# Eleven groups of a graph attention take their keys and values from node rows gathered early instead of from the table

## The chip, the cores and the metric

The kernel runs on one core of a Trainium2 chip. The metric is the device time in microseconds from the start of the program to its end. The engines are TensorE (PE, with its weight loads shown as PEld), VectorE (DVE), ScalarE (ACT), GpSimd (POOL) and SyncE (SP). Each works through its own queue in order, and they meet at semaphores.

## The reference

A graph of 3125 nodes (128 features, 8 heads of 16) has 100,000 edges, sorted by their destination, each of one of 5 relations. For every relation the edges attend within their destination node:

```python
for r in range(R):
    mask = edge_types == r
    q = jnp.einsum('eh,khd->ekd', x_dst, W_Q[r])
    k = jnp.einsum('eh,khd->ekd', x_src, W_K[r])
    v = jnp.einsum('eh,khd->ekd', x_src, W_V[r])
    logits = (q * k).sum(-1) / scale + attn_bias[r][None, :]
    masked_logits = jnp.where(mask[:, None], logits, NEG)
    max_v = jax.ops.segment_max(masked_logits, dst, num_segments=n)
    max_v = jnp.maximum(max_v, NEG)
    exp_l = jnp.where(mask[:, None], jnp.exp(masked_logits - max_v[dst]), 0.0)
    sum_exp = jax.ops.segment_sum(exp_l, dst, num_segments=n)
    attn = exp_l / (sum_exp[dst] + 1e-12)
    out = out + jax.ops.segment_sum(attn[:, :, None] * v, dst, num_segments=n)
out = out.reshape(n, HIDDEN)
out = out @ out_proj_w.T + out_proj_b
h = out + node_embeddings
mu = h.mean(-1, keepdims=True)
var = ((h - mu) ** 2).mean(-1, keepdims=True)
return (h - mu) / jnp.sqrt(var + LN_EPS) * ln_gamma + ln_beta
```

The caller adds the node features to this and normalizes once more. All is in 32-bit floats.

## The kernel before

The edges are cut into 196 groups of 512 (four tiles of 128 edges), the nodes into 25 blocks of 128. One block covers about 8 groups.

**First stage.** A loop over the 25 blocks makes a table `kv_d` in DRAM with the keys and values of every node under every relation. `turn` transposes a block of node rows, `table` multiplies it with the weights `wkv` in three f32 products (L312), ACT and DVE copy the results to SBUF (L316, L318) and SP stores them. Between the blocks stand pieces of bookkeeping, placed by the dictionary `side`: `begins` spreads the first destination of every group, `rows_of` finds for every node the row of sorted destinations in which it begins by comparing it with the first element of all 200 rows of 500, `in_row` gathers these rows (L341), and `count` counts on ACT how far into its row the node begins (L349). `keys_a` to `keys_c` and `along` make the indices `idx` and the keys of the edges.

**Second stage.** A loop over steps `k`. In step `k` one group `g` gets its logits, and one earlier group `v` gets its weights and sums. For a group:

- `gather` (POOL) fetches the 512 rows of `kv_d` with four indirect DMAs, three steps ahead (`AHEAD`), into one of `KVB` = 24 buffers.
- `fetch` (SP) loads the keys and a window of query rows; `spot` (DVE) makes a one-hot matrix of them; `spread_q` (PE, L603) multiplies the two, which gives each edge the query of its destination.
- `logits` (DVE, L616 and L617) multiplies keys and queries and reduces over each head; `store_logits` (SP) writes the result to `lg_d`.
- Later, for `v`: `spread_m` (PE) gives each edge its maximum, `less_max` (DVE) subtracts it, `exps` (ACT) exponentiates, `weigh` (DVE, L710) multiplies the values, `places` (ACT, L728 and L731) makes the one-hot matrix by destination, `sums` (PE, L744 to L754) adds up by destination, with the part that `carry` (ACT) took over from the group before, and `norm` (DVE) and `by_node` (ACT) divide and store.

For a block of nodes, once all of its groups have logits (step `full_step[b]`), `maxima_load` (POOL, L629) gathers the logits `ell` of each node from `lg_d` one step later. In the steps `ready[b]` - 5 and - 4, where `ready[b]` is `full_step[b]` plus `LAG` = 8 (6 for the last three blocks), `maxima` reduces them: ACT copies them by head into the PSUM tile `by_head` (L641), DVE forms `mine` (L643), `wl` (L656) and the maxima `mx` (L662). `store_m`, `fetch_m` then take the maxima to the groups, whose sums begin in step `ready[b]`. Sums run one group per step; `CATCH_UP` names five late groups that take two steps each, so that sums gain on the logits. `project`, `residual`, `roots` and `norms` finish a block, `queries` makes the query rows of a coming one.

The order on each engine is that of the program: in each step first the SP loads and stores, then POOL's gathers and `maxima_load`, then `residual`, `by_node` and `carry`, `spread_m`, `sums`, `spread_q`, and then the vector work, with `maxima`, `project`, `roots`, `norms` and `queries` last.

Of the kernel before, what the change touches and what calls it, by code (L numbers as in the profile page):

```python
# [17 lines left out]
P = 128  # L18
# [29 lines left out]
CATCH_UP = (186, 188, 190, 192, 194)  # L48
# [6 lines left out]
LAG = 8  # L55
SR = 500
NSR = E // SR
KVB = 24
# [58 lines left out]
def windowed_path(  # L117
# [13 lines left out]
    key_d = dram.tile([NGR, GE], BF16, name="key_d")  # L131

# [17 lines left out]
    wq = keep("wq", [P, R, H])  # L150

# [15 lines left out]
    nc.vector.memset(xn[:, NT - 1, :], 0.0)  # L167
    fr = load.tile([1, NGR + NSR], I32, name="fr")
# [16 lines left out]
    nc.sync.dma_start(xn[:, :4, :], x[: 4 * P].rearrange("(i p) h -> p i h", p=P))  # L185
# [7 lines left out]
    def load_rows(name, a, pad):  # L193
        t = load.tile([HG, 2, GE], I32, name=name)
        nc.vector.memset(t[:, 1, :], pad)
        nc.scalar.dma_start(t[:, 0, :], a[: HG * GE].rearrange("(g i) -> g i", i=GE))
        nc.scalar.dma_start(
            t[: HR - 1, 1, :], a[HG * GE : (NGR - 1) * GE].rearrange("(g i) -> g i", i=GE)
        )
        rest = E - (NGR - 1) * GE  # L200
        nc.gpsimd.dma_start(
            t[HR - 1 : HR, 1, :rest], a[(NGR - 1) * GE :].rearrange("(g i) -> g i", g=1)
        )
        return t
# [30 lines left out]
    mid = iota("mid", [[P * E // N, NT]], NT)  # L235
    five = iota("five", [[R, WN]], WN, mult=-1)
# [21 lines left out]


    wkv = load.tile([P, R, 2, H], F32, name="wkv")  # L260
# [14 lines left out]
    firsts = load.tile([P, NGR + NSR], F32, name="firsts")  # L275
    frf = load.tile([1, NGR + NSR], F32, name="frf")

    def begins():
        nc.vector.tensor_copy(frf, fr)
        fp = pps.tile([P, NGR + NSR], F32, name="fp", tag="tr", bufs=2)  # L280
        nc.tensor.matmul(fp, ones[0:1, :], frf, start=True, stop=True)
        nc.vector.tensor_copy(firsts, fp)
        nc.vector.tensor_copy(first, frf[:, :NGR])
        nc.vector.tensor_scalar_mul(first5, frf[:, :NGR], float(R))
        nc.vector.tensor_tensor(
            nkey[:, T, 1:], firsts[:, 1:NGR], firsts[:, : NGR - 1], op=ALU.subtract
        )
        nc.vector.tensor_scalar(
            nkey[:, T, 1:], nkey[:, T, 1:], float(R), row_of, op0=ALU.mult, op1=ALU.subtract
        )  # L290
# [35 lines left out]
    def rows_of(c0, c1):  # L326
        less = work.tile([P, 5, NSR], BF16, name="less", bufs=1)
        nc.vector.tensor_tensor(
            less,
            firsts[:, None, NGR:].to_broadcast([P, 5, NSR]),  # L330
            node[:, c0:c1, None].to_broadcast([P, 5, NSR]),
            op=ALU.is_lt,
        )
        g = grp[:, c0:c1]
        nc.vector.tensor_reduce(g, less, AX.X, ALU.add)
        nc.vector.tensor_scalar(g, g, 1.0, 0.0, op0=ALU.subtract, op1=ALU.max)
        nc.vector.tensor_copy(grp_i[:, c0:c1], g)
# [97 lines left out]
    def checks():  # L435
# [19 lines left out]
        1: [lambda: rows_of(0, 5)],  # L455
        2: [lambda: rows_of(5, 10), lambda: rows_of(10, 15)],
        3: [lambda: rows_of(15, 20)],
        4: [lambda: rows_of(20, NT)],
        5: [keys_a],
        6: [keys_c],  # L460
        7: [lambda: along(kvrow, 0, put_idx)],
        8: [lambda: along(kvrow, 1, put_idx)],
        9: [keys_b],
        11: [lambda: along(keyr, 0, put_key)],
        12: [lambda: along(keyr, 1, put_key)],
        13: [lambda: along(typr, 0, put_typ)],
        14: [lambda: along(typr, 1, put_typ)],
        16: [sorted_rows],
        18: [sorted_ends],
        21: [starts],  # L470
        23: [checks],
    }
    rows, counted = {}, 0
    xT = {b: turn(b) for b in range(2)}
    for b in range(NT):
        if b + 2 < NT:
            xT[b + 2] = turn(b + 2)
        table(b, xT.pop(b))
        for f in side.get(b, ()):
            f()  # L480
        while len(rows) < min(NT, 5 * b) and len(rows) - counted < 8:
            rows[len(rows)] = in_row(len(rows))
        for n in range(2):
            if b >= 3 and counted < len(rows):
                count(counted, rows[counted])
                counted += 1

# [39 lines left out]
    def gather(g):  # L527
        kv = kvs_[g % KVB]
        for t in range(T):
            nc.gpsimd.indirect_dma_start(  # L530
                out=kv[:, t, :], out_offset=None, in_=kv_d[:, :],
                in_offset=bass.IndirectOffsetOnAxis(ap=idx[:, t, g : g + 1], axis=0),
            )
# [49 lines left out]

    def fetch(g):
# [28 lines left out]
    def logits(g):  # L613
        kv, lg = kvs_[g % KVB], live["lg", g]
        prod = flow.tile([P, T, H], F32, name="prod")
# [20 lines left out]
    def maxima(b, c0, c1):  # L636
# [17 lines left out]
        wl = late_flow.tile([P, RH, HEADS, D], F32, name="wl", bufs=1)  # L654
# [200 lines left out]
    def lag(b):  # L855

        return LAG if b < NT - 3 else LAG - 2

# [18 lines left out]
    root_at[NT] = root_at[NT - 1] + 2  # L877

# [32 lines left out]
    for k in range(root_at[NT] + 2):  # L911
# [16 lines left out]
        for u in range(NGR):  # L928
            if max(at_k[u] - 3, ready[block_of(u)] - 2) == k:
                fetch_m(u)  # L930

# [6 lines left out]

        for b in range(NT):
# [47 lines left out]
        for b in range(NT + 1):  # L987
            if root_at[b] == k:
                roots(b)
                norms(b)  # L990
        if 0 in q_step:
# [510 lines left out]
```

## Time and profile before

| | |
|---|---|
| median of three runs | 1216.72 us (1213.73 to 1219.71) |
| the profiled execution | 1214.33 us, its span 1212.5 us |
| busy: PE, DVE, ACT, POOL | 799.7, 936.2, 728.9, 801.9 us |
| gathers of `kv` on POOL | 784, of 951 ns each, the first at 101.6 us, the last at 1130.7 us |
| first product of logits | 141.72 us |
| mean granted TensorE clock | 0.781 |
| DMA | 207.02 MB |

The page names an instruction group by its line, engine, operation and tiles. The waits list who waited for whom, with the total in microseconds, the number of times and the longest. The timeline gives start and duration of each instruction and, in brackets, the idle time of its engine before it with what ended it. Times in it count from the start of the span.

### The profile page before, as it was taken

How to read it: one execution, taken by the hardware profiler on the slowest of the kernel's cores; microseconds unless marked ns; L12 is line 12 of the kernel's file. 1: busy time of each engine (PE TensorE's matmuls, PEld its weight loads, DVE VectorE, ACT ScalarE, POOL GpSimd, SP SyncE). 2: the span in 40 equal slices, each digit the busy share in tenths (PEclk: the TensorE clock that was granted, in tenths of full speed). 3: DMA queues.
4: the chain of work that ended last, by engine and by line, in shares of the span. 5: the costliest groups of instructions: out<-in, count | busy, mean ns of one | idle time of the engine just before them, and what ended most of it. 6: DMA issues, size and time to landing. Idle time of an engine off the chain costs nothing.

```text
span 1212.5 us, 25279 instructions
## 1 busy us (share of the span) xinstructions
PE 799.7 (66%) x7503; PEld 690.8 (57%) x7503; DVE 936.2 (77%) x2521; ACT 728.9 (60%) x2441; POOL 801.9 (66%) x902
## 2 busy tenths in 40 slices
PE   5793346457576766767576666667765777568664
PEld 2351236457565665666466666557665666567664
DVE  4742375777888888788888888988888889877786
ACT  1562015357666756776777667667766776659443
POOL 2714777777777777777777777777777777774200
PEclk9996565778679776877988787878777888768767
DMA  6974787667567666776676667667666767654200
GB/s 168 336 315 144 220 214 178 152 181 191 157 175 178 178 169 179 183 177 162 182 192 167 167 183 187 164 175 184 178 168 168 195 166 178 170 138 117 67 9 14
DMA packets 181075, 207.02 MB, mean 171 GB/s; under 512 B 82614, under 2 KB 145871, under 8 KB 180808
## 3 DMA queue, kind: packets, MB, share of 16 engines
q0 software_dynamic: 41392, 116.59, 34.2%
q1 hardware_dynamic: 135112, 84.01, 27.8%
q10 hardware_dynamic: 4424, 4.71, 1.5%
q8 instruction: 62, 1.02, 0.3%
q14 instruction: 85, 0.70, 0.2%
HBM read 169.90 MB, written 35.29 MB: 169 GB/s over the span
## 4 chain that ended last, share of the span: by engine, by line
DVE 34%; DMA 22%; PE 14%; issue 10%; POOL 9%; ACT 9%; SPq 1%; DVEq 0%; ACTq 0%; POOLq 0%
DMA kv<-kv_d,idx 9%; POOL kv L530 9%; DMA ell<-lg_d,start_i 6%; DVE lg L617 5%; DVE prod L616 5%; DVE wv L710 4%; PE pp L744 4%; DVE wl L656 4%; PE pr L312 3%; ACT at L728 3%; DVE mx L662 2%; PE prq L556 2%; PE qe L603 2%; DVE hot L594 2%; DMA kt<-key_d 2%
## 5 line engine op out<-in xcount | busy, mean ns | idle before, releaser
L530 POOL DMA_INDIRECT kv<-kv_d,idx x784 | 745.4, 951 | 275.6 <-issue 195.7
L744 PE MATMUL pp<-wv,at 128*125 128x136 f32 x1568 | 300.6, 348 | 18.0 <-DVE o L769 15.9
L728 ACT ACTIVATE at<-row_at,nkey 128x125 f32<-128x125 f32 x934 | 292.0, 390 | 0.0
L744 PEld LDWEIGHTS pp<-wv,at 128*125 128x125 f32 x1568 | 255.1, 237 | 26.9 <-DVE o L769 18.3
L603 PE MATMUL qe<-qw,hot 125*128 125x128 bf16 x2352 | 208.3, 252 | 29.6 <-DVE hot L594 14.6
L603 PEld LDWEIGHTS <-hot 125*128 125x128 bf16 x2352 | 195.2, 124 | 35.4 <-DVE hot L594 22.7
L693 PE MATMUL me<-mw,hot 125*128 125x8 bf16 x2352 | 91.3, 168 | 184.1 <-DVE wv L710 124.4
L693 PEld LDWEIGHTS <-hot 125*128 125x128 bf16 x2352 | 83.2, 101 | 222.3 <-DVE wv L710 134.7
L704 ACT ACTIVATE me<-me 128x32 f32<-128x32 f32 x196 | 36.3, 185 | 218.6 <-DVE me L700 217.8
L616 DVE TENSOR_TENSOR prod<-kv,qe 128x512 f32<-128x512 f32 x196 | 134.1, 684 | 35.6 <-PE qe L603 17.6
L710 DVE TENSOR_TENSOR wv<-kv,me 128x512 f32<-128x512 f32 x196 | 133.1, 679 | 18.7 <-ACT wv L705 18.7
L731 ACT ACTIVATE at<-at 128x625 f32<-128x625 f32 (+2 forms) x196 | 137.5, 702 | 6.2
L617 DVE TENSOR_REDUCE lg<-prod 128x32 f32<-128x512 f32 x196 | 134.4, 686 | 6.8
L748 PE MATMUL pp<-pt,at 125*125 125x136 f32 x390 | 100.6, 347 | 35.3 <-ACT pt L760 35.3
L556 PE MATMUL prq<-wq,xTq 128*128 128x384 f32 (+1 forms) x100 | 59.1, 688 | 81.5 <-DVE rem L566 80.3
L748 PEld LDWEIGHTS pp<-pt,at 125*125 125x125 f32 x390 | 77.5, 242 | 41.6 <-ACT pt L760 40.9
L594 DVE TENSOR_SCALAR hot<-kt,row_of 125x512 bf16<-125x512 bf16 x196 | 72.2, 368 | 15.9 <-DMA kt<-key_d 15.8
L656 DVE TENSOR_TENSOR wl<-by_head,shut 128x1536 f32<-128x1536 f32 (+1 forms) x50 | 74.5, 1491 | 8.2 <-ACT by_head L641 6.5
L754 PEld LDWEIGHTS pp<-rsum,o 125*128 125x128 f32 x392 | 78.2, 243 | 2.8 <-issue 2.0
L662 DVE TENSOR_REDUCE mx<-wl 128x24 f32<-128x1536 f32 (+1 forms) x50 | 74.3, 1486 | 1.7
L556 PEld LDWEIGHTS prq<-wq,xTq 128*128 128x128 f32 x100 | 22.5, 279 | 90.7 <-DVE rem L566 88.6
L754 PE MATMUL pp<-rsum,o 125*128 125x25 f32 x392 | 70.5, 263 | 2.6 <-DVE o L769 1.9
(158 smaller groups left out, 1000.5 us busy)
## 6 DMA issues: line engine op xcount, KB each, us to landing
kt<-key_d SPq DMA_DIRECT2D x196, 128.0 KB
qw<-q_d SPq DMA_DIRECT2D x196, 96.0 KB
kv_d<-kvs SPq DMA_DIRECT2D x24, 640.0 KB
kv<-kv_d,idx POOLq DMA_INDIRECT x784
q_d<-q SPq DMA_DIRECT2D x25, 480.0 KB
lg_d<-lg SPq DMA_DIRECT2D x196, 18.0 KB
mw<-m_d SPq DMA_DIRECT2D x196, 6.0 KB
xq<-in_x SPq DMA_DIRECT2D x24, 64.0 KB
```

The source lines that it names most:

```text
L530: nc.gpsimd.indirect_dma_start(out=kv[:, t, :], out_offset=None, in_=kv_d[:, :], in_offset=bass.IndirectOffsetOnAxis(ap=idx[:, t, g : g + ...
L603: nc.tensor.matmul(qe[:, t, :], hot[:, t, :], qw[:WR, s, :], start=(s == 0), stop=(s == 2))
L616: nc.vector.tensor_tensor(prod, kv[:, :, :H], live.pop(("qe", g)), op=ALU.mult)
L617: nc.vector.tensor_reduce(lg[:, :, :HEADS], prod.rearrange("p t (k d) -> p t k d", d=HD), AX.X, ALU.add)
L656: nc.vector.tensor_tensor(wl[:, :n], by_head[:, None].to_broadcast([P, n, HEADS, D]), shut[:, :n, None, :].to_broadcast([P, n, HEADS, D]), ...
L693: nc.tensor.matmul(me[:, t, :], hot[:, t, :], mw[:WR, s, :], start=(s == 0), stop=(s == 2))
L710: nc.vector.tensor_tensor(wv[:, :, :H].rearrange("p t (k d) -> p t k d", d=HD), kv[:, :, H:].rearrange("p t (k d) -> p t k d", d=HD), live ...
L728: nc.scalar.activation(at[:, t, :], row_at[:, :WR], AF.Abs, bias=nkey[:, t, g : g + 1], scale=1.0)
L731: nc.scalar.activation(at[:, on_dve:n, :], at[:, on_dve:n, :], AF.Relu, bias=1.0, scale=-1.0)
L744: nc.tensor.matmul(pp, at[:, t, :], wv[:, t, :], start=(t == 0), stop=(t == T - 1 and g == 0))
L748: nc.tensor.matmul(pp, at[:WR, T, :], live.pop(("pt", g - 1)), start=False, stop=True)
L754: nc.tensor.matmul(op, live.pop(("o5", done)), rsum[:WR], start=True, stop=True)
```

## The change

Of the groups 6, 22, 38, ... 166 (`XG`, eleven groups) the four gathers from the table are left out. Instead the 512 source rows of the node features `x` are gathered by `early_x` (POOL, 44 indirect DMAs of 128 rows of 512 bytes) during the first stage: 16 before the loop over blocks, one after each block from the third on, the rest after the loop. `put_x` (SP) stores a group's rows to `x_d` in DRAM, five groups within the loop and six after it.

In the second stage such a group is prepared over seven steps from `x_at[g]` - 2 on. `x_at[g]` is the group's step less 5, or earlier, so that the PSUM tile shared with `maxima` is free. `fetch_types` and `fetch_early` load the relations of the edges, spread over all partitions, and the rows; `turn_x` transposes the rows (PE); `by_relation` makes of them five copies, each zero where the edge has another relation (DVE); `products` multiplies each copy with that relation's weights and adds the five up (PE, twice for two tiles each); `put_kv` copies the result into the group's `kv` buffer (ACT). From there on the group goes as all others do.

Further: `LAG` is 7, the last three blocks keep 6, and `CATCH_UP` is empty. `KVB` is 23. `rows_of` works once for all nodes on rows of 250, and compares the nodes of a block with 48 rows near the place where they begin on average. The loads of `dst`, `edge_type` and `src` rows go from ACT's queue to SP's, the first load of `x` goes ahead, `warm` is an early small copy on ACT, and the tile `prod` has one buffer.

```diff
-CATCH_UP = (186, 188, 190, 192, 194)
+CATCH_UP = ()
-LAG = 8
-SR = 500
+LAG = 7
+SR = 250
+SB = P * E // N // SR
+SPAD = 5
+XG = range(6, 167, 16)
-KVB = 24
+KVB = 23
...
-        nc.scalar.dma_start(t[:, 0, :], a[: HG * GE].rearrange("(g i) -> g i", i=GE))
-        nc.scalar.dma_start(
+        nc.sync.dma_start(t[:, 0, :], a[: HG * GE].rearrange("(g i) -> g i", i=GE))
+        nc.sync.dma_start(
...
+    def rows_of():
+        less = load.tile([P, NT, 3, SB], F32, name="less")
+        rows = firsts.rearrange("p (b s) -> p b s", s=SB)
+        for i in range(3):
+            nc.vector.tensor_tensor(
+                less[:, :, i, :], rows[:, i : i + NT, :],
+                node[:, :, None].to_broadcast([P, NT, SB]), op=ALU.is_lt,
+            )
+        nc.vector.tensor_reduce(grp, less.rearrange("p b i s -> p b (i s)"), AX.X, ALU.add)
...
+    def early_x():
+        i, t = pieces.pop(0)
+        if t == 0:
+            staged[i] = work.tile([P, T, H], F32, name="xg", bufs=6)
+        nc.gpsimd.indirect_dma_start(
+            out=staged[i][:, t, :], out_offset=None, in_=x[:, :],
+            in_offset=bass.IndirectOffsetOnAxis(ap=xi[:, i, t : t + 1], axis=0),
+        )
+
+    def put_x(most):
+        for i in sorted(staged)[:most]:
+            nc.sync.dma_start(x_d[i], staged.pop(i).rearrange("p t h -> p (t h)"))
+
+    for n in range(16):
+        early_x()
...
-        while len(rows) < min(NT, 5 * b) and len(rows) - counted < 8:
+        while b >= 1 and len(rows) < NT and len(rows) - counted < 8:
             rows[len(rows)] = in_row(len(rows))
+        if b >= 2:
+            early_x()
+            put_x(1 if len(pieces) % T < T - 2 and b % 2 else 0)
...
+    while pieces:
+        early_x()
+    put_x(len(XG))
...
     def gather(g):
+        if g in XG:
+            return
...
+    def fetch_types(g):
+        tr = flow.tile([P, GE], I32, name="tr", bufs=1)
+        nc.sync.dma_start(tr, edge_type[g * GE : (g + 1) * GE].partition_broadcast(P))
+        live["tr", g] = tr
+
+    def fetch_early(g):
+        xe = flow.tile([P, T, H], F32, name="xe", bufs=1)
+        nc.sync.dma_start(xe.rearrange("p t h -> p (t h)"), x_d[XG.index(g)])
+        live["xe", g] = xe
+
+    def turn_x(g):
+        xe = live.pop(("xe", g))
+        tx = ps.tile([P, T, P], F32, name="tx", tag="by_head", bufs=1)
+        for t in range(T):
+            nc.tensor.transpose(tx[:, t, :], xe[:, t, :], ident)
+        live["tx", g] = tx
+
+    def by_relation(g):
+        tr, tx = live.pop(("tr", g)), live.pop(("tx", g))
+        xm = late_flow.tile([P, R, T, P], F32, name="xm", tag="wl", bufs=1)
+        for r in range(R):
+            nc.vector.scalar_tensor_tensor(
+                xm[:, r], tr.rearrange("h (p t) -> h t p", t=T), float(r), tx,
+                op0=ALU.is_equal, op1=ALU.mult,
+            )
+        live["xm", g] = xm
+
+    def products(g, t0):
+        xm = live["xm", g]
+        pk = ps.tile([P, 2, KVW], F32, name="pk", tag="by_head", bufs=1)
+        for t in range(2):
+            for r in range(R):
+                nc.tensor.matmul(
+                    pk[:, t, :], xm[:, r, t0 + t, :], wkv[:, r].rearrange("h s c -> h (s c)"),
+                    start=(r == 0), stop=(r == R - 1),
+                )
+        if t0:
+            live.pop(("xm", g))
+        live["pk", g] = pk
+
+    def put_kv(g, t0):
+        nc.scalar.copy(kvs_[g % KVB][:, t0 : t0 + 2, :], live.pop(("pk", g)))
...
-        return LAG if b < NT - 3 else LAG - 2
+        return LAG if b < NT - 3 else LAG - 1
...
+    for g in XG:
+        k = step_of[g] - 5
+        while any(k < m + 1 and k + 4 > m for m in (r - 5 for r in ready)):
+            k -= 1
+        x_at[g] = k
...
+        for u in XG:
+            if x_at[u] + 3 == k:
+                put_kv(u, 0)
+            if x_at[u] + 4 == k:
+                put_kv(u, 2)
         for b in range(NT):
             if done_at[b] + 1 == k:
                 residual(b)
...
+        for u in XG:
+            if x_at[u] == k:
+                turn_x(u)
+            if x_at[u] + 1 == k:
+                by_relation(u)
+            if x_at[u] + 2 == k:
+                products(u, 0)
+            if x_at[u] + 3 == k:
+                products(u, 2)
         if 0 in q_step:
             turn_q(q_step[0])
```

## The prediction

> **What bounds the kernel now.** I read the page first, then the windows, the waits, and the timelines of all engines over one block of 128 nodes. The page's busy shares and its costliest group:
>
> ```profile
> PE 799.7 (66%) x7503; PEld 690.8 (57%) x7503; DVE 936.2 (77%) x2521; ACT 728.9 (60%) x2441; POOL 801.9 (66%) x902
> L530 POOL DMA_INDIRECT kv<-kv_d,idx x784 | 745.4, 951 | 275.6 <-issue 195.7
> ```
>
> No engine is full, but the POOL timeline shows gather after gather with 0.30 us between:
>
> ```profile
> 626.38 0.95 POOL L530 DMA_INDIRECT kv<-kv_d,idx  x1 [0.30 <-issue]
> 627.63 0.95 POOL L629 DMA_INDIRECT ell<-lg_d,start_i  x1 [0.30 <-issue]
> 628.88 0.94 POOL L530 DMA_INDIRECT kv<-kv_d,idx  x1 [0.30 <-DVE me L700]
> ```
>
> One gather is 1.25 us, a group of four 5.0, and this runs from 101.6 to about 1106 us. So POOL sets the pace. What counts is how far behind it the next limit lies. That is in the waits (us in total, times, longest):
>
> ```profile
> ACT by_head L641 <- DMA ell<-lg_d,start_i: 51.6, 22, 7.8
> DVE mine L643 <- DMA ell<-lg_d,start_i: 42.2, 22, 4.5
> DVE prod L616 <- DMA kv<-kv_d,idx: 14.1, 7, 4.3
> ```
>
> DVE hardly waits for a gathered `kv` itself: of the 14.1 us 8.6 lie up to group 20. In steady state it meets POOL at one place per block, the `ell` gather, which stands in POOL's queue behind the gathers of later groups. There it waits 42.2/22 = 1.92 us per block of 8 groups. From the product (L616) of group 20 at 210.91 us to that of group 184 at 1065.63 are 854.7 us, 20.5 blocks of 41.7. So the rest of the machine (DVE with PE and ACT in lockstep; I call it the compute side) needs 41.7 - 1.9 = 39.8 per block. POOL is first by 5% only.
>
> The block's timelines show why PE and ACT belong to that side (start, duration, engine, line):
>
> ```profile
> 660.73 1.19 PE L744 MATMUL pp<-wv,at 128*125 128x136 f32 x8 [0.18 <-DVE o L769]
> 662.13 0.83 PE L603 MATMUL qe<-qw,hot 125*128 125x128 bf16 x12
> 665.08 0.30 ACT L812 ACTIVATE sd<-mv,eps_t 128x2 f32<-128x2 f32 x1
> 665.41 0.17 DVE L817 RECIPROCAL sd<-sd 128x2 f32<-128x2 f32 x1 [1.33 <-ACT sd L812]
> 672.05 0.73 ACT L731 ACTIVATE at<-at 128x625 f32<-128x625 f32 x1
> 674.46 1.08 ACT L641 COPY by_head<-ell 128x512 f32<-128x512 f32 x1 [1.67 <-DMA ell<-lg_d,start_i]
> ```
>
> **A rule against this reading.** The windows give DVE 42.39 us busy of 50:
>
> ```profile
> 650.00:700.00 50.00, 36.99 (x389) 34.23 (x388) 42.39 (x117) 34.89 (x122) 37.89 (x40) 0.79 0.68 173
> ```
>
> The Trainium skill ("Trainium Kernel Development and Optimization", Best Practices, item 5) tells one to judge TensorE by its weight loads and says "other engines: occupancy is fine". By occupancy DVE has 15% of some 1030 us free, 155 us; all the new vector work (34 us, below) would fit, POOL would stay the bound, and the sum would be about 1160. By the wait row only 42 us are free, because the other gaps of DVE are waits inside the lockstep (square root 1.33, `qe` 0.98, `wv` 0.61 per block). I take the row.
>
> **The change, part by part.** An "early group" is one of the 11 (6, 22, ... 166).
>
> *POOL.* 44 of 784 gathers leave the loop: 44 x 1.25 = 55 us. In the stretch from group 20 to 184, ten early groups save 50.
>
> *Early groups, DVE.* `by_relation` adds five 128x512 multiplies with a compare. Nearest rows: `prod`, 0.68 with an operand in PSUM, and the 99x1024 integer one (L379) at 1.22; independent neighbours start 0.60 to 0.69 apart. 5 x 0.62 = 3.1 us, 34 for all. They end iteration x_at+1 and nothing there hides them.
>
> *Early groups, PE.* `turn_x` is four transposes (25 in the table stage take 0.11 each in the chain), under 1 us in an iteration with room. `products` twice makes ten f32 products of 256 columns. The table stage, at a granted clock of 0.97, has 1280 columns in
>
> ```profile
> 70.64 2.15 PE pr L312 x6
> ```
>
> that is 1.68 ns a column: 0.43 us each, 4.3 per call, 8.6 per group. (The row mean of 392 ns per record would give 15.7; records overlap, so I use starts.)
>
> *Early groups, ACT.* `put_kv` is a 128x512 copy, 0.58 by L316, but it is the first instruction of its iteration on ACT and waits for PE's products. Behind it stand `by_node`, `carry` (PE's last `pp` needs it), `exps` (DVE's `weigh` needs it) and `places`.
>
> *The walk.* `x_at` is the group's step minus 7 for ten of the eleven, so the second products call comes in the iteration before a block's `maxima`. I lay it on the traced block, whose corresponding iterations lie at 658 to 674 us. DVE is late by 3.1 from the first. First products: they follow the multiplies, about 664 to 667; ACT is then busy with places and the square root (`sd` at 665.38, now 668.5), so this call is hidden. Next iteration: copy and carry end at 669.6, PE finishes `qe` at 671.1, second products to 675.4. Next: ACT's second copy waits for that, so `exps` starts at 676.6, where 670.07 + 3.1 = 673.2 was due; `places` ends at 679.3, and `by_head` follows. In the trace `places` ended at 672.78. So an early group costs the compute side **6.5 us**, 3.1 of DVE and 3.4 of waiting. Lower end 3.1 (all of PE and ACT hidden); upper end 10, if products run at half clock.
>
> *The clock, a second rule.* Eight `pp` records take 1.19 us at 660.73 and 2.17 at 640.28, after PE had idled 3.30: a factor of two. "TensorE: Matmul & The Clock Gate" (Part 1) says that an idle window of some 3.4 us brings half clock. The gap before the first products is about 1.1 us (662.96 to 664), so I take full clock; if the multiplies stretch that gap over the rule's window, the calls begin at 8.6 instead of 4.3, p becomes about 10, and nine groups add 32 us more.
>
> *LAG 7.* Maxima come one iteration earlier after the block's last group. The trace's `ell` lands 5.3 us after its start, the store of the logits takes about 2.7 before: 8.0 after the last logits. DVE arrives about 10.6 after them (rest of that iteration 1.6, roots and norms 3.1, two iterations of 2.95). It fits by 2.6 once the compute side is the slower. Between 0 and 1.9 (as now) per block; I take 0.4, near 0 because of that slack. Queued behind this wait are DVE's next product and ACT's next copies; `store_m` on SP waits for its result, and `mw` for that.
>
> *CATCH_UP empty.* Last sum step 214 becomes 213; five sums move behind the last logits, in the same number. One step of sums alone is 2.55 us (`weigh` of groups 190 to 195): -3.
>
> *SP in the loop.* Two loads of 256 KB per early group, two iterations ahead, replace four gathers of 128 KB; issues of 0.35 us each: 0, since SP waits for logits anyway. KVB 23, one buffer less and one lag less: the slot is free two steps ahead as before, 0. `prod` single: both its users are on DVE, 0.
>
> *Start.* The search on DVE goes from 5 x 2.75 = 13.7 to three 128x400 compares and one reduction, about 3.7 by the 128x396 copies (0.57) and L335; PE waited some 5 of these 10 us. Row loads leave ACT's queue, which issued until 15.95: the first table product, at 18.38, some 4 earlier. `sign` halves its row (ACT -6, covered). Against this POOL gets 44 gathers, 55 us, into its waits of 21.5 and 36.9: 58.4, so they just fit; the queue ends near 98 to 103, the first `kv` gather now starts at 101.6. SP gets eleven stores; the last six stand before the query loads: 0 to 5. DMA moves 5.8 MB more and 3.2 less, 0 to 8 at 312 GB/s. Net between -6 and +8; I take +2.
>
> **Sum** (profiled execution, 1214.3, span 1212.5).
> - To group 20: the five waits before it hold 11.9 us (0.2, 4.3, 3.2, 3.0, 1.2). Compute side: 210.9 - 11.9 + 2 x 6.5 + 2 = 214.0; POOL would allow 206. +3.
> - Group 20 to 184: 854.7 - 39.4 (waits for `ell`) + 9 x 6.5 + 20.5 x 0.4 = 882; POOL 805. +27.
> - End: -3.
>
> 1214.3 + 27 = 1241.3. The median of the runs, 1216.7, is 2.4 above that execution: 1244.
>
> **The rivals.**
> *Faster: the products hide.* If ACT and PE take the new work in their own gaps, an early group costs the compute side only 3.1. Then the long stretch is 854.7 - 39.4 + 28 = 843, the start -4, the end -3: 1198, or 1206 with 0.4 of `ell` wait per block. It decides at a price p of 4.0 us per early group (11p = 39.4 - 8 + 9.9 + 3). For: PE's weight loads fill 57% only. Against: `put_kv` at the head of ACT's iteration. 0.14.
> *POOL stays the bound.* The occupancy reading: -55, about 1160. Against: the 1.92 us. 0.06.
> *Gain and price cancel*, p near 4: 1211 to 1223. 0.09.
> *Half clock.* p = 10 and `ell` waits of 1 per block: 854.7 - 39.4 + 90 + 20 = 925, start +12: 1296; with half of that excess 1270. 0.15.
> *My forecast*, p from 4.5 to 8: 1223 to 1265. 0.56.
> *The early gathers do not save POOL time* (POOL waits for `ell` anyway): part of the forecast, for then the compute side sets the pace.
>
> **The numbers.** Within 0.5% (about what a measurement of this kernel can tell from no change) 0.09; slower 0.56 + 0.15 = 0.71; faster 0.20. The range 1199 to 1284 reaches from the hidden case to the middle of half clock; it leaves out the full gain, the lowest hidden cases and the dearest half-clock ones, under 2 in 10.
>
> **What would show it.** The waits for `ell` on DVE fall from 42 us to under 20, and POOL's 0.30 us rhythm breaks: 740 gathers, with waits of several us before `ell` that end with a logits store. DVE gets 55 new rows near 0.69. ACT gets 22 copies of 128x512, half of them after waits of 1 to 3 us for PE's `pk`. Wrong: POOL still at 0.30 from end to end with `ell` waits kept, or the iterations around the products no longer than now.

## The result, and the profile after

The changed kernel takes 1318.6 us (median of 4 runs, 1312.4 to 1326.6) beside 1215.35 for the kernel before on the same chip: 1.0847 times as long, with a 95% interval of 1.0781 to 1.0913. The forecast was 1244, in a range of 1199 to 1284.

The profiled execution has a span of 1317.0 us, 104.5 more than before. The page's busy shares and its gathers now:

```profile
PE 912.4 (69%) x7989; PEld 785.4 (60%) x7989; DVE 981.7 (75%) x2577; ACT 730.7 (55%) x2452; POOL 800.4 (61%) x903
L583 POOL DMA_INDIRECT kv<-kv_d,idx x740 | 703.5, 951 | 306.6 <-issue 185.6
```

POOL's gathers of `kv` are 42 us shorter, DVE is busy 45.5 us longer and PE 113. The waits (who waited for whom: us in total, times, longest) that answer to those shown of before:

```profile
POOL kv L583 <- DVE den L864: 79.6, 37, 4.3
ACT kv L680 <- PE pk L671: 64.8, 19, 28.5
ACT by_head L739 <- DMA ell<-lg_d,start_i: 44.9, 14, 6.3
DVE mine L741 <- DMA ell<-lg_d,start_i: 37.0, 15, 3.9
```

POOL is no longer the bound: it stands 79.6 us before the `kv` gathers because their buffers are still in use (the row names `den`, which DVE makes behind `weigh`, the last reader of a buffer). Yet DVE waits for `ell` almost as long as before, 37.0 us against 42.2. That pair is the puzzle of this case. The timeline of the stretch in which group 86 is prepared (start, duration, engine, line; idle time before it in brackets):

```profile
588.89 4.95 DVE L660 SCALAR_TENSOR_TENSOR xm<-tr,tx 128x512 f32<-128x512 int32 x5
593.99 4.55 PE L671 MATMUL pk<-wkv,xm 128*128 128x256 f32 x20 [1.99 <-DVE me L798]
598.59 0.58 ACT L680 COPY kv<-pk 128x512 f32<-128x512 f32 x1 [0.30 <-PE pk L671]
600.09 0.94 POOL L727 DMA_INDIRECT ell<-lg_d,start_i  x1 [6.04 <-ACT pt L858]
600.74 4.54 PE L671 MATMUL pk<-wkv,xm 128*128 128x256 f32 x20
605.31 0.58 ACT L680 COPY kv<-pk 128x512 f32<-128x512 f32 x1 [1.86 <-DMA kv<-kv_d,idx]
606.50 0.69 DVE L808 TENSOR_TENSOR wv<-kv,me 128x512 f32<-128x512 f32 x1 [2.27 <-ACT me L802]
```

The five multiplies take 4.95 us, not 3.1. The products of this group take 4.55 each, near the 4.3 foreseen. ACT's second copy starts 0.03 us after the second products end (its bracket names a DMA, but the order of times shows what it stood behind), `exps` follows the copy, and DVE waits 2.27 for it. POOL stood still for 6.04 us before its `ell`.

Not all products ran like these. Of the eleven first calls, four took 4.55 us and seven 6.0 to 6.3 (two of the seven are split in the trace), while all second calls took 4.54 to 4.58. Two first calls in the windows (stretch; its length; busy time of PE, PEld, DVE, ACT, POOL; granted clock; DMA share; GB/s):

```profile
408.17:414.31 6.14, 6.14 (x27) 5.08 (x27) 4.40 (x16) 4.21 (x11) 3.01 (x4) 0.74 0.53 144
501.72:506.27 4.55, 4.55 (x27) 3.94 (x28) 2.88 (x9) 4.21 (x11) 1.09 (x2) 1.00 0.69 223
```

The granted clock is 0.72 to 0.75 in the seven and 1.00 in the four. While DVE multiplies, PE idles before the first call: 2.3 to 3.3 us before five of the slow ones, 0.9 to 2.0 before the four. Before the other two, of groups 6 and 38, PE's last matmuls were slow already (2.77 and 1.45 us instead of 0.83).

### The profile page after: what moved, and what is told of

Its sections match the earlier page's. It is cut to its first block, busy times and chain, and to the rows that moved or that the text cites. A ratio compares the mean times of both kernels' runs of the same rounds, so it can differ in the third digit from the quotient of the medians.

```text
span 1317.0 us, 26391 instructions
## 1 busy us (share of the span) xinstructions
PE 912.4 (69%) x7989; PEld 785.4 (60%) x7989; DVE 981.7 (75%) x2577; ACT 730.7 (55%) x2452; POOL 800.4 (61%) x903
## 4 chain that ended last, share of the span: by engine, by line
DVE 39%; PE 20%; DMA 17%; ACT 9%; issue 9%; POOL 3%; SPq 2%; DVEq 0%; ACTq 0%; POOLq 0%
PE pk L671 6%; DVE wl L754 5%; DVE lg L715 5%; DVE prod L714 4%; DVE wv L808 4%; DMA ell<-lg_d,start_i 4%; PE pp L842 4%; DVE xm L660 4%; DMA kv<-kv_d,idx 3%; ACT at L826 3%; DVE mx L760 2%; POOL kv L583 2%; PE pr L336 2%; PE qe L701 2%; DMA mw<-m_d 2%
## 5 line engine op out<-in xcount | busy, mean ns | idle before, releaser
L583 POOL DMA_INDIRECT kv<-kv_d,idx x740 | 703.5, 951 | 306.6 <-issue 185.6
L842 PE MATMUL pp<-wv,at 128*125 128x136 f32 x1568 | 307.2, 353 | 24.1 <-DVE o L867 21.1
L826 ACT ACTIVATE at<-row_at,nkey 128x125 f32<-128x125 f32 x922 | 288.6, 390 | 0.0
L842 PEld LDWEIGHTS pp<-wv,at 128*125 128x125 f32 x1568 | 260.8, 242 | 33.5 <-DVE o L867 18.5
L701 PE MATMUL qe<-qw,hot 125*128 125x128 bf16 x2352 | 200.6, 247 | 27.4 <-DVE hot L692 16.0
L791 PE MATMUL me<-mw,hot 125*128 125x8 bf16 x2352 | 90.7, 168 | 179.1 <-DVE wv L808 145.2
L791 PEld LDWEIGHTS <-hot 125*128 125x128 bf16 x2352 | 82.5, 100 | 220.6 <-DVE wv L808 163.2
L701 PEld LDWEIGHTS <-hot 125*128 125x128 bf16 x2352 | 189.3, 121 | 30.8 <-DVE hot L692 17.9
L802 ACT ACTIVATE me<-me 128x32 f32<-128x32 f32 x196 | 36.9, 188 | 259.3 <-DVE me L798 257.4
L671 PE MATMUL pk<-wkv,xm 128*128 128x256 f32 x440 | 111.6, 414 | 26.5 <-DVE me L798 24.0
L671 PEld LDWEIGHTS pk<-wkv,xm 128*128 128x128 f32 x440 | 90.1, 209 | 42.0 <-issue 27.3
L846 PEld LDWEIGHTS pp<-pt,at 125*125 125x125 f32 x390 | 77.5, 242 | 45.1 <-ACT pt L858 45.0
L754 DVE TENSOR_TENSOR wl<-by_head,shut 128x1536 f32<-128x1536 f32 (+1 forms) x50 | 74.5, 1491 | 14.8 <-ACT by_head L739 13.7
L727 POOL DMA_INDIRECT ell<-lg_d,start_i x25 | 23.7, 949 | 101.5 <-DMA qw<-q_d 19.6
```

Of the source, the lines that this page charges most:

```text
L583: nc.gpsimd.indirect_dma_start(out=kv[:, t, :], out_offset=None, in_=kv_d[:, :], in_offset=bass.IndirectOffsetOnAxis(ap=idx[:, t, g : g + ...
L671: nc.tensor.matmul(pk[:, t, :], xm[:, r, t0 + t, :], wkv[:, r].rearrange("h s c -> h (s c)"), start=(r == 0), stop=(r == R - 1),)
L701: nc.tensor.matmul(qe[:, t, :], hot[:, t, :], qw[:WR, s, :], start=(s == 0), stop=(s == 2))
L754: nc.vector.tensor_tensor(wl[:, :n], by_head[:, None].to_broadcast([P, n, HEADS, D]), shut[:, :n, None, :].to_broadcast([P, n, HEADS, D]), ...
L791: nc.tensor.matmul(me[:, t, :], hot[:, t, :], mw[:WR, s, :], start=(s == 0), stop=(s == 2))
L826: nc.scalar.activation(at[:, t, :], row_at[:, :WR], AF.Abs, bias=nkey[:, t, g : g + 1], scale=1.0)
```

## The experiments

I measured each variant by its own trace as well: from the start to the logits product of group 20, from there to that of group 184 ("the stretch"), and the rest. Before has 210.9, 854.7 and 146.9 us; after has 244.95, 929.1 and 142.9.

**The parts of the change, without early groups.** First all of the change but the early groups (`no_early_b`): no rows gathered early, nothing prepared.

```diff
-XG = range(6, 167, 16)
+XG = ()
```

> The changed kernel without early groups once more, on another chip: in the first job the kernel before itself took 1642 us, with waits of some 10 us per block that the profile gives to no engine or queue of this core, and which neither trace of the two kernels has. If those are gone, theory 1 (the preparation of the early groups costs the compute side about 10 us a group, the rest is near neutral) expects the stretch from group 20 to 184 at 845 to 862 us, the first product at 138 to 150, the whole 1205 to 1230; theory 2 (LAG 7 with one buffer less costs by itself, through longer waits for ell) expects a stretch above 890 and the whole above 1255.

1232.65 us, 1.0129 (1.0109 to 1.0149) times the kernel before. To group 20: 220.4, the stretch 866.1, just above the range of the first theory and far below the second's. So the rest of the change costs 1.3% and the early groups about 7%. Next, in `search_and_queues`, the lag, the buffers and the slowed steps also go back:

```diff
-XG = range(6, 167, 16)
-LAG = 7
-KVB = 23
-CATCH_UP = ()
+XG = ()
+LAG = 8
+KVB = 24
+CATCH_UP = (186, 188, 190, 192, 194)
```

> No early groups, and lag 8, 24 buffers and the five slowed steps at the end as in the kernel before: what is left of the change is the search over near rows, the queues of the loads and the order of the table phase. Without early groups but with lag 7 and 23 buffers the time is 1232.65, and it loses 9.7 us between group 18 and 20 and 11.4 from group 20 to 184, where a maximum or its ell comes late. If lag 7 and the 23 buffers cost these, this variant takes 1212-1219 and group 20 comes at 209-212. Rival: the order of the table phase costs them (ell of block 0 or q of the first blocks late): 1225-1234, group 20 still at 218-221.

1214.05 us, 0.9979 (0.9962 to 0.9996); group 20 at 210.0, the stretch 854.0. The search and the queues by themselves gain at most a few microseconds. Lag or buffers cost the difference; `lag7_24_buffers` is `no_early_b` with the 24th buffer given back (`KVB = 24`):

> No early groups, lag 7 and no slowed steps, but 24 buffers. With lag 7 and 23 buffers it is 1232.65, with lag 8, 24 buffers and the slowed steps 1214.05. If lag 7 costs the difference, 1228-1235, group 20 again near 220; if the missing buffer does, 1213-1218, group 20 near 210.

1234.88 us, 1.0118 (1.0082 to 1.0154), group 20 at 221.1, the stretch 868.7. It is the lag, not the buffer. (The slowed steps come behind group 184, where this variant loses nothing: 145.2 us against 146.5.)

**What the gathers taken out are worth.** `relief_only_c` keeps the gathers of rows in the first stage and leaves out all that follows from them in the second (two buffers that nothing fills are cleared once; the cut shows one line of each kind):

```diff
-                fetch_types(u)
-                fetch_early(u)
...
-                put_kv(u, 0)
...
-                turn_x(u)
...
-                by_relation(u)
...
-                products(u, 0)
```

> Leaves out what the early groups' second half does (the loads of types and node rows, the transposes, multiplies, products and copies; the keys and values of the 11 groups are wrong), and keeps the 44 gathers taken out of the ring, with the node-row gathers of the table phase. If GpSimd sets the pace wherever compute is not in its way, the stretch from group 20 to 184 falls from 866 without early groups to 815-835, total about 1195-1215. Rival: the gathers taken out are worth little even with no work put in their place, because the ring of buffers, the waits for ell and the schedule set the pace: the stretch stays at 850-866, total 1220-1235.

1244.72 us, 1.0224 (1.0179 to 1.027). The stretch is 864.4: forty gathers fewer, and 1.7 us gained on `no_early_b`. The rival was right here: taken alone, with lag 7, the relief is worth nothing. (The total lies above both ranges because of the start, below.) Is this the compute side's own pace, or the lag? `relief_lag8` has lag 8, 24 buffers and the slowed steps:

```diff
-CATCH_UP = ()
-LAG = 7
-KVB = 23
+CATCH_UP = (186, 188, 190, 192, 194)
+LAG = 8
+KVB = 24
```

> As the relief alone (the second half of the early groups left out, the keys and values of the 11 groups wrong, 44 gathers fewer), but with lag 8, 24 buffers and the five slowed steps of the kernel before. With lag 7 the relief gave 1.7 us over the stretch from group 20 to 184 (864.4 against 866.1). If it was lag 7 that ate the relief (the maxima wait for the round trip of the logits through DRAM, however early GpSimd is free), the stretch falls now from 854 to 818-832 and the total to 1190-1203 (the table phase keeps its 12.7). Rival: the vector, scalar and tensor engines need 41-42 us for a block by themselves, so that no gather taken away is ever worth anything: the stretch stays at 848-856, total 1218-1228.

1200.75 us, 0.9874 (0.9841 to 0.9907), the stretch 821.1. The same relief now gives 32.8 us there against `search_and_queues` (853.95 less 821.14). DVE's wait for `ell` in the profiles of the two, first lag 7:

```profile
DVE mine L744 <- DMA ell<-lg_d,start_i: 63.5, 25, 6.1
```

then lag 8:

```profile
DVE mine L744 <- DMA ell<-lg_d,start_i: 10.3, 8, 2.6
```

Why can lag 7 not be met even with POOL relieved? In the timeline of `relief_only_c`, group 81 is the last that a block needs. Its logits are reduced by 553.8:

```profile
552.03 0.34 SPq L690 DMA_DIRECT2D qw<-q_d  x1
553.16 0.69 DVE L718 TENSOR_REDUCE lg<-prod 128x32 f32<-128x512 f32 x1
555.83 0.34 SPq L635 DMA_DIRECT2D q_d<-q  x1
557.13 0.57 SPq L723 DMA_DIRECT2D lg_d<-lg  x1
563.47 0.94 POOL L730 DMA_INDIRECT ell<-lg_d,start_i  x1 [2.32 <-DMA xq<-in_x]
567.30 0.33 DVE L744 SCALAR_TENSOR_TENSOR mine<-slot,deg,ell 128x64 f32<-128x64 f32 x1 [2.78 <-DMA ell<-lg_d,start_i]
```

SP issues the logits' store 3.3 us after they are there: in the same step the 480 KB of query rows (`q_d`) stand ahead of it in SP's order and are issued first. And that store is late itself, since SP stands waiting before it. SP's own waits name for what, a load of query rows (`qw`) that was issued shortly before:

```profile
SPq L635 <- DMA qw<-q_d: 71.7, 22, 4.7
```

POOL, idle for 2.32, issues `ell` late, and DVE waits 2.78. (POOL's bracket names another load; the experiment that follows shows that the order of the two stores decides.) In the 14 blocks that I compared below (last groups 49 to 153) the query store always falls into that step. `q_store_behind` changes nothing but this order in `relief_only_c`, lag 7 kept:

```diff
-        if 5 in q_step:
-            store_q(q_step[5])
...
             store_logits(g)
+        if 5 in q_step:
+            store_q(q_step[5])
```

> The relief alone with lag 7 (second half of the early groups left out, their keys and values wrong), and one thing moved: in its step the store of the query rows (480 KB) is issued behind the store of the logits instead of ahead of it. In the relief with lag 7 the logits of a block's last group are stored 4.3 to 5.3 us after their product begins, those of the group before 1.47 after, because the query store of that step stands ahead on SP and waits; ell follows 4.8 after the store, and VectorE waits 2.2 per block for it. If this order is what eats the relief, that wait falls to under 0.6 per block, the stretch from group 20 to 184 from 864.4 to 821-840, and the total from 1244.7 to 1200-1222. Rival: the step taken from the lag is itself too much (DMA round trip and gather alone are longer than two steps), or the query rows come too late: the stretch stays above 855 and the total above 1235.

1210.55 us, 0.9948 (0.9921 to 0.9974), the stretch 832.2: 32.2 of the 43.3 us between lag 7 and lag 8 are back. Means over 14 blocks from the traces, in us after the start of the product of the block's last group:

| | its logits stored | `ell` issued | DVE arrives | DVE waits |
|---|---|---|---|---|
| `relief_only_c`, lag 7 | 4.73 | 9.48 | 11.92 | 2.17 |
| `relief_lag8` | 3.65 | 9.12 | 14.98 | 0.23 |
| `q_store_behind`, lag 7 | 1.48 | 6.97 | 11.87 | 0.43 |

The cause of the lost relief is the order on SP together with the shorter lag: either the store goes first, or DVE comes one step later. The 11 us that `q_store_behind` stays behind lag 8 have their place in other blocks: over the whole stretch DVE waits 45.9 us for `ell` in `relief_only_c`, 16.6 in `q_store_behind` and 5.9 in `relief_lag8`, and 8.6 of the 16.6 are in the first three blocks. Why these still wait stays open.

In the changed kernel itself, in the same 14 blocks, the pattern of `relief_only_c` stands in every second block: there the logits are stored 4.2 to 5.2 us after the product's start, and DVE waits 1.3 to 3.2 us in six of these seven. In the seven between them an early group's products fall into that step, the query store is issued before the step's product starts, the logits are stored after 1.5, and DVE waits for nothing. So its total, 37.0, comes near that of before, but for another reason. The whole change with the store moved was not tried.

**What an early group costs.** `one_multiply_d` makes one of the five masked copies and lets all five products use it:

```diff
-        for r in range(R):
+        for r in range(1):
             nc.vector.scalar_tensor_tensor(
...
-                    pk[:, t, :], xm[:, r, t0 + t, :], wkv[:, r].rearrange("h s c -> h (s c)"),
+                    pk[:, t, :], xm[:, 0, t0 + t, :], wkv[:, r].rearrange("h s c -> h (s c)"),
```

> One of the five relation multiplies of each early group is made and used by all five products (keys and values of the 11 groups are wrong). In the trace of the changed kernel the step in which the multiplies stand is 4.8 us longer than the same step of the variant without early groups, and the five multiplies take 4.95. If they lie bare, four fewer save 3.96 for each of 11 groups: 40 to 48 us, total 1270-1280. Rival: the burst is paid elsewhere (the products and the copy into the buffer bind next, or GpSimd takes over): under 20 us are saved, total over 1298.

1286.16 us, 1.0565 (1.0463 to 1.0667), the two runs at 1276.6 and 1295.7; the median misses the range by 6 us, and the trace is that of the faster run. In it the stretch is 887.8, 41.3 us shorter than after's for nine groups with four multiplies fewer: 4.6 per group, a little more than the 3.96 that the instructions take. By the medians it is 32.4 us for eleven groups, or 2.9 each. So the multiplies lie bare, all or most of them; the lengths of the steps below say the same. With one multiply PE no longer idles before the first products, and of their eleven calls all but the first group's take 4.54.

`five_forms` gives the groups five forms of the multiply in turn:

```diff
+        xe, form = live.pop(("xe", g)), XG.index(g) % 5
+        strided, plain = tr.rearrange("h (p t) -> h t p", t=T), tr.rearrange("h (t p) -> h t p", t=T)
...
+            if form == 4:
+                nc.vector.tensor_tensor(xm[:, r], xe, tx, op=ALU.mult)
+            else:
+                nc.vector.scalar_tensor_tensor(
+                    xm[:, r], plain if form in (1, 3) else strided, float(r),
+                    xe if form in (2, 3) else tx, op0=ALU.is_equal, op1=ALU.mult,
+                )
```

> The 11 early groups take five forms of the multiply in turn (their keys and values are wrong for four of the five): 0, as in the change: types with a stride of 4 elements from SBUF against tx in PSUM (0.99 us); 1, the types contiguous, against PSUM; 2, strided types against the node rows in SBUF; 3, contiguous types against SBUF; 4, a plain TENSOR_TENSOR multiply of the SBUF rows by tx in PSUM, float32. The prediction took 0.62 from a TENSOR_SCALAR row of the same size. If the strided integer operand costs the rest, forms 1 and 3 take 0.6-0.7 and form 2 0.99; if the PSUM operand does, forms 2 and 3 are short and 4 is long; if it is the instruction with two operations, forms 0 to 3 all take 0.99 and form 4 takes 0.68, like the product of the logits (0.68). Total near 1318 less at most 10.

It ran on a chip whose total tells nothing (below), but the durations of DVE's instructions stand. Its timeline, five multiplies of one group in each line, forms 0 to 4 in order:

```profile
210.66 4.93 DVE L665 SCALAR_TENSOR_TENSOR xm<-tr,tx 128x512 f32<-128x512 int32 x5
297.15 3.07 DVE L665 SCALAR_TENSOR_TENSOR xm<-tr,tx 128x512 f32<-128x512 int32 x5
418.35 5.05 DVE L665 SCALAR_TENSOR_TENSOR xm<-tr,xe 128x512 f32<-128x512 int32 x5
528.96 3.13 DVE L665 SCALAR_TENSOR_TENSOR xm<-tr,xe 128x512 f32<-128x512 int32 x5
640.23 3.07 DVE L663 TENSOR_TENSOR xm<-xe,tx 128x512 f32<-128x512 f32 x5
```

Only the stride matters: 4.93 and 5.05 with types read four elements apart, 3.07 and 3.13 with the types side by side. Whether the other operand lies in PSUM or SBUF changes it by 0.12 at most, and the plain multiply with one operation takes the same 3.07.

`after_lag8` is the whole change with lag 8 and the slowed steps (23 buffers: a 24th does not fit beside the masked copies).

```diff
-CATCH_UP = ()
-LAG = 7
+CATCH_UP = (186, 188, 190, 192, 194)
+LAG = 8
```

> The whole change, early groups and all, with lag 8 and the slowed steps, and 23 buffers as changed (a 24th does not fit beside the five masked copies). If lag 7 costs the changed kernel what it costs the variant without early groups (18.6), this is 1296-1303. Rival: beside the early groups' own work the wait for ell is covered half of the time, and lag 8 with 23 buffers makes GpSimd wait for buffers: 1308-1325.

1298.58 us, 1.0661 (1.0621 to 1.07), the stretch 912.5. Beside `relief_lag8` it prices the early groups when little waits for `ell` (7.8 us in all): 91.4 us for the nine groups prepared in the stretch, 10.2 each (2.4 of the 91.4 are a last step of group 22). Mean lengths of the steps from `x_at` on, over eight groups:

| step after `x_at` | 0 | 1 | 2 | 3 | 4 |
|---|---|---|---|---|---|
| `relief_lag8` | 4.69 | 2.92 | 5.77 | 3.33 | 7.92 |
| `after_lag8` | 4.75 | 7.79 | 5.66 | 4.45 | 10.73 |

Step 1 is longer by 4.87, the multiplies. Steps 3 and 4 are longer by 1.12 and 2.81, where the copies wait for the products and ACT's other work waits for the copies. The five steps together are longer by 8.75; the rest of the 10.2 was not placed.

The slow first calls show in step 3. In this trace, of the nine groups prepared in the stretch, three have a first call of 4.55 us at a granted clock of 1.00, and their step 3 is shorter than in `relief_lag8` by 0.1 to 1.0; six have one of 6.0 to 7.55 us at 0.60 to 0.76, and their step 3 is longer by 1.2 to 3.0. So the 1.12 goes with the clock, as far as the traces tell; no run changes the clock alone. Step 4 is longer in both kinds. POOL's wait for buffers in the profile:

```profile
POOL kv L583 <- DVE den L864: 106.7, 39, 8.7
```

This wait does no harm that the trace shows: DVE waits for a gathered `kv` only 4.8 us, twice. POOL has time to spare, and the other engines use it up.

**The start.** `no_group_6_b` prepares ten groups, 22 to 166:

```diff
-XG = range(6, 167, 16)
+XG = range(22, 167, 16)
```

> Ten early groups instead of eleven: the first is 22, so that no preparation lies in the first iterations; the rest as changed. If the 24.5 us that the start loses against the variant without early groups (group 20 at 244.95 against 220.4) lie mostly in group 6's bare preparation, group 20 comes at 222-230 and the total falls to 1296-1303. Rival: they lie in the table phase (weights later by 7.3, the x_d stores and gathers before xq, first product at 156 against 142): group 20 stays at 233-242 and the total is 1306-1314.

1305.7 us, 1.0725 (1.0673 to 1.0777), group 20 at 237.2. Group 20 falls into the range of the rival, the table stage, but group 6 is still worth 7.7 us of the start. In `relief_only_c`, where nothing is prepared, group 20 comes at 233.5, still 13.1 later than in `no_early_b`. Of that 12.7 are there at the first product (154.93 against 142.21). The traces show two places. The table's last products begin at 97.0 instead of 89.0; the last of POOL's row gathers `dr`, which stand among the early ones, begins at 77.5 instead of 65.2. And SP loads the first query rows behind the stores of `x_d`. `no_early_b`:

```profile
99.76 0.33 SPq L581 DMA_DIRECT2D xq<-in_x  x1
```

`relief_only_c`:

```profile
104.74 5.70 SPq L513 DMA_DIRECT2D x_d<-xg  x6
114.77 0.33 SPq L597 DMA_DIRECT2D xq<-in_x  x1
```

The two were not tried apart; which share each has stays open.

**Runs that did not settle it.** Nine runs came from two chips on which the kernel before itself takes 1625 to 1642 us, so that their totals measure another limit. The mean granted clock of before is 0.66 to 0.69 there, against 0.76 to 0.77 in most of its runs on the other chips. The first four had these expectations: no early groups,

> The changed kernel without early groups: all 784 gathers back, no early_x, no put_x, no preparation in the loop; search, queues, LAG 7, empty CATCH_UP and 23 buffers stay. Theory 1 (the preparation of the early groups costs the compute side about 10 us a group, and the rest is near neutral): the stretch from group 20 to 184 is back at 845 to 862 us (after: 929), the first product at 138 to 150, the whole 1205 to 1230. Theory 2 (LAG 7 with one buffer less costs by itself, through longer waits for ell): the stretch stays above 890, the whole above 1255.

the relief alone,

> The changed kernel with the gathers of the eleven groups left out and nothing in the loop in their place (these groups compute with stale keys and values); early_x and put_x stay. It shows what the relief of POOL is worth by itself. Theory 1 (the compute side needs 39.8 us per block): stretch 815 to 835 us, 20 to 40 below before, and not the 50 that POOL saves; whole 1195 to 1220, since the start stays late. Theory 2 (POOL was the only bound): stretch near 805. Theory 3 (POOL gives the relief back in waits for buffers or for ell whatever else runs): stretch 845 or more.

one multiply of five,

> Only one of the five multiplies by relation per early group, its result read by all products; the values of the early groups are wrong for it, all else is unchanged. Theory 1 (vector work lies bare on the compute side): 4 x 0.99 us less per group, 11 groups: -40 to -48, whole 1270 to 1280, stretch about 890. Rival (the prepared products and the copies behind them carry the price, the multiplies hide): less than 15 us gained.

and one product instead of five for each tile (`for r in range(1)` in `products`):

> Two instead of ten products per call (one relation of five); the values of the early groups are wrong for it, all else is unchanged. Theory 1 (products hide except for a tail before the maxima, and at group 6): -1.5 to -2.5 us in each of ten groups and about -10 at group 6, whole 1285 to 1300. Rival, the prediction's own split (3.4 us of waiting behind products per group): -35 or more, whole below 1283.

They took 1633.05, 1598.94, 1637.57 and 1633.88 us beside 1641.96 before: 0.993 (0.9906 to 0.9955), 0.9729 (0.9706 to 0.9753), 0.9976 (0.9949 to 1.0002) and 0.9956 (0.9942 to 0.9969). `relief_only_b` (0.9731, 0.9689 to 0.9773), `one_multiply_b` (0.9968, 0.995 to 0.9985), `one_multiply_c` (0.998, 0.9964 to 0.9997) and `no_group_6` (1.0047, 1.0026 to 1.0069) repeated this, with the expectations that their successors above carry in much the same words; `five_forms` took 1640.56 beside 1638.52. `five_forms` is a single run. The relief shows there, the cost of an early group does not. What the products cost by themselves was not measured on another chip and stays open.

## Why the prediction was wrong

Four of the profiles make a chain from before to after, each with one more part of the change. The differences, in us:

| | to group 20 | the stretch | the rest | sum |
|---|---|---|---|---|
| search, queues (`search_and_queues`) | -0.9 | -0.8 | -0.3 | -2.0 |
| gathers out of the loop, rows gathered early (`relief_lag8`) | +14.5 | -32.8 | +3.5 | -14.8 |
| early groups prepared (`after_lag8`) | +11.1 | +91.4 | -4.6 | +97.9 |
| lag 7, no slowed steps (after) | +9.4 | +16.6 | -2.6 | +23.4 |
| all | +34.0 | +74.4 | -4.0 | +104.5 |
| forecast | +3 | +27 | -3 | +27 |

The shares depend on the order in which the parts are added. The lag, for one, costs the stretch 14.7 us without early groups (868.7 less 854.0, with 24 buffers), 43.3 in the relieved variant, and 16.6 in the full one, where the early groups' work covers part of the wait.

- **POOL first by 5%, the compute side 39.8 us per block: right.** `relief_lag8` runs the stretch in 821.1, which is 40.05 per block of 20.5. This also decides against the occupancy reading: with 40 gathers away the stretch gives 33 us and not the 50 that POOL would allow, though DVE was 77% busy. The term "-39.4" was -32.8, since of the waits for `ell` only 36.9 us lie in the stretch and 5.9 stay.
- **Five multiplies at 0.62: this step failed.** They take 4.95 us, bare in the step in which they stand. The price was taken by size, from rows of other instructions; `five_forms` shows that the stride of four elements costs the 1.9 us. The stride stands in the diff, `tr` rearranged by "(p t)", and the prediction did not price it.
- **Waiting behind products and copies, 3.4 us: near, in part by luck.** 3.9 in the two steps with lag 8, of which 1.1 go with the slow first calls that the prediction left out. Its gap of 1.1 us before the first products became 0.9 to 3.3, because the multiplies are longer; seven of the eleven first calls took 6.0 to 6.3 us, none the 8.6 of half clock, and one slow call came after a gap of 2.3, well under the 3.4 us of the prediction's rule, with full clock before it. The rival "half clock", with a price of 10, had the price that was measured (10.2), but mostly for another reason: about 1.1 of the 10.2 go with the clock. Of the 3.7 by which 6.5 fell short the stride makes half, the waiting 0.5, and 1.4 were not placed.
- **LAG 7, 0.4 us per block: this step failed.** In the full kernel it is 0.8 per block (16.6 over 20.5), in the relieved one 2.1. "DVE arrives about 10.6 after them" holds (11.9 from the product's start, which is 10.5 from the last logits). "The store about 2.7 before" does not: `ell` starts 8.1 after the last logits in `relief_only_c`, because the store comes 4.7 after the product starts, not 1.5, with the query store ahead of it on SP. Even with the store moved it is 5.6, so the term was half its size at best. Before has the late store already, as its timeline and waits on SP show:

```profile
SPq L579 <- DMA qw<-q_d: 59.8, 21, 4.7
532.58 0.34 SPq L589 DMA_DIRECT2D qw<-q_d  x1
535.05 0.34 SPq L579 DMA_DIRECT2D q_d<-q  x1
536.35 0.39 SPq L622 DMA_DIRECT2D lg_d<-lg  x1
```

  The mean there is 3.5 us from product to store at those steps, and 1.5 at the steps before them. With lag 8, and `ell` not started before 11.3 because POOL is the bound, no wait of POOL or DVE named the store; that moving it would gain nothing there was not tried. SP's own waits named the place.
- **The start, +3: this step failed, by 31 us.** The sum had +2 for the table stage and -11.9 for five waits that would end, -9.9 together; measured are +13.6 (-0.9 and +14.5). The gain from the search, which at the low end was to make the net -6, is -0.9. The stores before the query loads were put at 0 to 5, and POOL's early gathers at "just fit"; with them the first product comes at 157.3 in `relief_lag8`, 16.2 later than in `search_and_queues`, and only 1.7 of that is won back by group 20. The lag's 9.4 in this part was not in the sum either. The two groups prepared before group 20 were not the error: they cost 11.1, and the sum had 13.
- **The end, -3: right** (-4.0).
- **What it said would be seen.** 740 gathers, 55 new DVE rows (0.99 instead of 0.69), 22 copies, and POOL's broken rhythm: seen. Of the copies 19 and not half waited for `pk`, one of them for 28.5 us (that of group 6). `ell` waits of DVE under 20: not with lag 7 (37.0), but with lag 8 (7.8 over five waits in `after_lag8`).

The direction was right since an early group costs more than its four gathers can give: with lag 8, 10.2 against 3.3 (32.8 over ten groups). By these figures multiplies of 3.1 with nothing waiting behind them would just have broken even in the stretch, and the start would still have been lost; that is an estimate, not a run.

Of the variants that leave nothing out, `search_and_queues` is the fastest, at 0.9979 (0.9962 to 0.9996) of before; that is less than the half per cent that this kernel's measurement tells from no change.

## What to carry to other kernels

When the engine that sets the pace is relieved, what the relief is worth ends at the next limit; measure that limit by leaving the work out and putting nothing in its place, with all else as in the tuned kernel. When a lag is shortened, follow the one transfer on which the awaited value depends through its queue in that very step, since a store that is late there is covered as long as the lag is long. The waits of the engine that needs the value need not name it; look at the waits of the queue that issues the transfer. Price a vector instruction by a row with the same access pattern, not only the same size.

## What the runs showed of the hardware

- A 128x512 multiply on DVE with an int32 operand read with a stride of four elements takes 0.99 us from one to the next, 0.62 when it lies side by side (4.95 and 3.07 to 3.13 for five). An operand in PSUM instead of SBUF changed the five by 0.12 at most (`five_forms`).
- The ten products of a call took 4.55 us at a granted clock of 1.00 and 6.0 to 6.3 at 0.72 to 0.75 (after). In `after_lag8` the same PE idle time of 2.98 us stood before calls of 4.55 and of 6.24, so in these traces it does not tell which of the two follows.
- On the two slower chips PE often gets single matmuls with pauses that no instruction explains, while POOL gathers without a break. From `relief_only_b`:

```profile
311.20 0.39 PE L845 MATMUL pp<-wv,at 128*125 128x136 f32 x1 [1.72 <-issue]
313.34 0.38 PE L845 MATMUL pp<-wv,at 128*125 128x136 f32 x1 [1.75 <-issue]
```

  Eight such records take 1.19 us together in the trace of before. What delays PE there was not found.
